# A convolution stage fed from strips of taps, with four images loaded side by side, logits in four column groups and a last batch scaled by two engines

## The chip, the cores and the metric

The kernel runs on one core of a Trainium2 chip. The core has four computing engines: TensorE (PE, matrix products; the profile lists its weight loads apart, as PEld), VectorE (DVE), ScalarE (ACT) and GpSimd (POOL), and SyncE (SP), which here issues most of the DMA transfers. Every engine takes its instructions strictly in the order of its own queue and waits on semaphores for the others. The metric is the device time of one execution in microseconds (us), lower is better. Before the change it is 16079.44 us, the median of three runs (16073.9 to 16081.61).

## What is computed

Two layers on `x` of shape (32, 128, 56, 56), all in float32. The change touches only the first lines of the first layer:

```python
x = conv_general_dilated(input, dw_kernel, (1, 1), ((3, 3), (3, 3)), feature_group_count=C) + dw_bias
x = transpose(x, (0, 2, 3, 1))                                   # one token of 128 channels per pixel
x = (x - mean(x)) / sqrt(var(x) + 1e-06) * ln_gamma + ln_beta    # over the channels
logits = x.reshape(T, C) @ Wg + bg                               # 8 experts
topv, topi = top_k(logits, 2)
...                                                              # routing, experts, and the second layer
```

So: a 7x7 convolution of each channel by itself, a normalization over the channels of each pixel, and eight logits per pixel, of which the two largest are found. Routing by priority with a capacity, the experts, and a second layer with a state-space scan follow.

## The kernel before

**Tiling.** The 32 images go in 8 batches of 4 (`NB0`). Rows of an image are taken in pairs: 2 rows of 56 pixels are 112 partitions (`TT`), and there are 28 pairs (`NP`). An image comes in with channels on partitions; `fill` (L341) loads it into one buffer `xt`, turns it with 29 transposes on PE (L349, `p_in`, four to a PSUM tile, two tiles) and ACT copies the result (L351) into `slots2`, of which there are two, for even and odd batches: [112 pixels, channel, image and row pair].

**Convolution.** `conv(b, c0)` (L353) does 4 channels of 4 images: for each channel four products (L379) over 112 pixels of an input row pair, with a 112 x 112 block of a band matrix that holds the 7x7 taps. 16 such matmuls are called a *group* here; a batch has 32 groups. A float32 matmul is two instructions on PE, each with its own weight load, so a group is 32 instructions. DVE adds the bias and writes back to `slots2` (L383); `pc` has three PSUM buffers. In the first batch the blocks are made: windows of the taps are loaded from `taps_d` with overlapping reads (`raw`, L361), copied by ACT to a dense form (L368), and stored by POOL's queue to `toep_d` (L369). Later batches load the dense form from there (L371, two loads of 392 KB per group, five buffers).

**Normalization.** `norm(b, i, q)` (L388) treats seven row pairs of one image; 16 calls make a batch. DVE takes statistics (L396, L398), ACT the root (L400), DVE the reciprocal and the shift `nm` (L401, L403). ACT scales seven times, one row pair each (L406: the *scalings*). POOL multiplies by gamma and adds beta (L409, L410) in `xa`, which has three buffers. SP stores `xa` to `res_d` (L412). PE turns `xa` (L420, seven transposes), ACT copies that (L422, two copies), PE computes the logits with seven products of 112 rows by 8 columns (L424), DVE adds the bias (L428). `top2` (L430) closes a batch on DVE.

**Order.** While batch b is convolved, batch b-1 is normalized and batch b+1 is filled. The loop over `k` at the end of the stage writes these calls in turn; a scheduler of the framework then orders the instructions of every engine when the program is built. Within an engine nothing changes at run time. After the last batch, 16 norms run with no convolution beside them. The stage ends with the last `top2`; routing, dispatch, experts and `layer1` (whose order is written out by hand in `PLAN` and `UNITS`) follow.

Of the kernel before, what the change touches and what calls it, by code (L numbers as in the profile page):

```python
# [5 lines left out]
F32 = mybir.dt.float32  # L6
# [14 lines left out]
E = 8  # L21
# [223 lines left out]
def tile_kernel(tc: tile.TileContext, a: dict, out: bass.AP):  # L245
# [14 lines left out]
    with (  # L260
# [43 lines left out]
        with (  # L304
# [4 lines left out]
            tc.tile_pool(name="po1", bufs=2, space=PSUM) as pot,  # L309
            tc.tile_pool(name="pl1", bufs=1, space=PSUM) as plg,  # L310
        ):
            wg = wp.tile([C, E], F32, name="wg")
            nc.sync.dma_start(out=wg, in_=a["L0_conv_Wg"])

            def rows(v, n, name):
                t = wp.tile([TT, n], F32, name=name)
                nc.sync.dma_start(out=t, in_=v.partition_broadcast(TT))
                return t

            bg = rows(a["L0_conv_bg"], E, "bg")  # L320
# [1 line left out]
            lng = rows(a["L0_conv_ln_gamma"], C, "lng0")  # L322
            lnb = rows(a["L0_conv_ln_beta"], C, "lnb0")

            taps_d = dram.tile([C, TR * TS], F32, name="taps_d")
            toep_d = dram.tile([TT, C, 8, HW], F32, name="toep_d")
            slots2 = [wp.tile([TT, C, NB0 * (NP + 1)], F32, name=f"xc{i}") for i in range(2)]  # L330

            xt = wp.tile([C, (HW + 2) * HW], F32, name="xt")
            nc.gpsimd.memset(xt, 0.0)
            taps = xt[:, : TR * TS].rearrange("c (y x) -> c y x", x=TS)
            dwk = a["L0_conv_dw_kernel"].rearrange("c o h w -> (c o) h w")
            for y in range(7):
                nc.sync.dma_start(out=taps[:, 7 - y, 52:59], in_=dwk[:, y, :])
            nc.sync.dma_start(out=taps_d, in_=xt[:, : TR * TS])
            nc.gpsimd.memset(xt[:, :HW], 0.0)

            def fill(b, i):  # L341

                n = b * NB0 + i
                nc.sync.dma_start(out=xt[:, HW : HW + L], in_=x_d[n])
                for j0 in range(0, NP + 1, 4):
                    w = min(4, NP + 1 - j0)
                    p = pin.tile([TT, 4, C], F32, name="p_in")
                    for j in range(w):
                        nc.tensor.transpose(p[:, j, :], xt[:, (j0 + j) * TT : (j0 + j + 1) * TT], ident)  # L349
                    o = i * (NP + 1) + j0  # L350
                    nc.scalar.copy(slots2[b % 2][:, :, o : o + w], p[:, :w, :].rearrange("p j c -> p c j"))  # L351

            def conv(b, c0):  # L353

                tp = []
                for c in range(c0, c0 + 4, 2):
                    t = cp.tile([TT, 2, 8, HW], F32, name="toep", bufs=5)
                    if b == 0:
                        raw = cp.tile([TT, 2, 8, TS], F32, name="raw", tag="xa", bufs=3)
                        for r in range(2):  # L360
                            nc.sync.dma_start(  # L361
                                out=raw[r * HW : (r + 1) * HW].rearrange("k c y x -> k c (y x)"),
                                in_=bass.AP(
                                    tensor=taps_d.tensor, offset=c * TR * TS + (1 - r) * TS,
                                    ap=[[1, HW], [TR * TS, 2], [1, 8 * TS]],
                                ),
                            )
                        nc.scalar.copy(t, raw[:, :, :, :HW])  # L368
                        nc.gpsimd.dma_start(out=toep_d[:, c : c + 2], in_=t)  # L369
                    else:  # L370
                        nc.sync.dma_start(out=t, in_=toep_d[:, c : c + 2])  # L371
                    tp.append(t)
                s4 = slots2[b % 2][:, c0 : c0 + 4, :].rearrange("p c (i j) -> p c i j", i=NB0)
                pc = pconv.tile([TT, 4, NB0, NP], F32, name="pc")
                for c in range(4):
                    for k, o in enumerate((1, 2, 0, 3)):

                        lo, hi = max(0, 1 - o), min(NP, NP + 2 - o)
                        nc.tensor.matmul(  # L379
                            pc[:, c, :, lo:hi], lhsT=tp[c // 2][:, c % 2, 6 - 2 * o : 8 - 2 * o, :],  # L380
                            rhs=s4[:, c, :, lo + o - 1 : hi + o - 1], start=k == 0, stop=k == 3,
                        )
                nc.vector.tensor_tensor(  # L383
                    s4[:, :, :, :NP].rearrange("p c i j -> p c i j"), pc,
                    dwb[:, c0 : c0 + 4].unsqueeze(2).unsqueeze(3).to_broadcast([TT, 4, NB0, NP]), ALU.add,
                )

            def norm(b, i, q):  # L388

                w = NP // 4  # L390
                o = i * (NP + 1) + q * w
                xv = slots2[b % 2][:, :, o : o + w]
                st = cp.tile([TT, w, 6], F32, name="st")
                mv = cp.tile([TT, w, 2], F32, name="mv")
                for j in range(w):
                    nc.vector.bn_stats(st[:, j, :], xv[:, :, j])  # L396
                for j in range(w):
                    nc.vector.bn_aggr(mv[:, j, :], st[:, j, :])  # L398
                rs = cp.tile([TT, w], F32, name="rs")
                nc.scalar.activation(rs, mv[:, :, 1], AF.Sqrt, bias=eps6[:TT])  # L400
                nc.vector.reciprocal(rs, rs)  # L401
                nm = cp.tile([TT, w], F32, name="nm")
                nc.vector.scalar_tensor_tensor(nm, mv[:, :, 0], -1.0, rs, ALU.mult, ALU.mult)  # L403
                xa = cp.tile([TT, 2 * 8 * TS], F32, name="xa", bufs=3)[:, : w * C].rearrange("p (j c) -> p j c", c=C)
                for j in range(w):
                    nc.scalar.activation(  # L406
                        xa[:, j, :], xv[:, :, j], AF.Identity, bias=nm[:, j : j + 1], scale=rs[:, j : j + 1]
                    )
                nc.gpsimd.tensor_tensor(xa, xa, lng.unsqueeze(1).to_broadcast([TT, w, C]), ALU.mult)  # L409
                nc.gpsimd.tensor_tensor(xa, xa, lnb.unsqueeze(1).to_broadcast([TT, w, C]), ALU.add)  # L410
                col = (b * NB0 + i) * TPI + q * w
                nc.sync.dma_start(  # L412
                    out=res_d[col * TT : (col + w) * TT, :].rearrange("(k p) c -> p k c", p=TT), in_=xa
                )
                pl = plg.tile([TT, w, E], F32, name="p_lg")
                for j0 in range(0, w, 4):
                    g = min(4, w - j0)
                    p = pot.tile([C, 4, TT], F32, name="p_xa")
                    for j in range(g):
                        nc.tensor.transpose(p[:, j, :], xa[:, j0 + j, :], ident[:TT, :TT])  # L420
                    xc = cp.tile([C, 4, TT], F32, name="xc_lg")
                    nc.scalar.copy(xc[:, :g, :], p[:, :g, :])  # L422
                    for j in range(g):
                        nc.tensor.matmul(pl[:, j0 + j, :], lhsT=xc[:, j, :], rhs=wg, start=True, stop=True)  # L424
                if i == 0 and q == 0:
                    lgs[b] = cp.tile([TT, NB0 * TPI, E], F32, name="lg")
                o = i * TPI + q * w
                nc.vector.tensor_tensor(lgs[b][:, o : o + w, :], pl, bg.unsqueeze(1).to_broadcast([TT, w, E]), ALU.add)  # L428

            def top2(b):  # L430

                n = NB0 * TPI
                big = [TT, n, E]
                cols = slice(b * n, (b + 1) * n)
                lg = lgs.pop(b)
                oh = cp.tile(big, F32, name="oh", bufs=1)
                first_b = first.unsqueeze(1).to_broadcast(big)
                v = cp.tile([TT, 2, n], F32, name="v", bufs=1)
                for k in range(2):
                    nc.vector.tensor_reduce(v[:, k, :], lg, AX.X, ALU.max)  # L440
                    nc.vector.tensor_tensor(oh, lg, v[:, k, :].unsqueeze(2).to_broadcast(big), ALU.is_equal)
                    nc.vector.tensor_tensor(oh, oh, first_b, ALU.mult)
                    nc.vector.tensor_reduce(picks[k][:, cols], oh, AX.X, ALU.max)
                    if k == 0:
                        nc.vector.tensor_tensor(
                            oh, first_b, picks[k][:, cols].unsqueeze(2).to_broadcast(big), ALU.is_equal
                        )
                        nc.vector.scalar_tensor_tensor(lg, oh, -3.0e38, lg, ALU.mult, ALU.add)
                nc.vector.tensor_tensor(less[:, cols], v[:, 1, :], v[:, 0, :], ALU.subtract)
# [992 lines left out]
```

## Time and profile before

| stretch of the profiled execution | us | what runs |
|---|---|---|
| 0 to 69 | 69 | constants, taps, four images loaded and turned |
| 69 to 249 | 180 | convolution of batch 0 |
| 249 to 1238 | 989 | batches 1 to 6: convolution, norms, fills |
| 1238 to 1390 | 152 | batch 7: convolution, norms of batch 6 |
| 1390 to 1535 | 145 | norms of batch 7 |
| 1535 to 16084 | 14549 | all the rest |

The profiled execution took 16086.15 us, with a span of 16084.4 us from its first to its last instruction on the core, at a mean granted TensorE clock of 0.888; the three unprofiled runs have their median at 16079.44 us. Over the span PE is busy for 13000.1 us, DVE 11071.4, ACT 11045.9, POOL 13580.1.

How to read the lines that follow: a timeline line has start, duration, engine, source line, operation, output <- inputs, shapes, and how often it follows itself; in brackets the idle time of the engine before it and what ended that. A row of a stretch has its bounds and length, the busy time of PE, PEld, DVE, ACT and POOL with the number of instructions, the granted TensorE clock as a share of full speed, the mean busy share of 16 DMA engines, and GB/s.

### The profile page before, as it was taken

How to read it: one execution, taken by the hardware profiler on the slowest of the kernel's cores; microseconds unless marked ns; L12 is line 12 of the kernel's file. 1: busy time of each engine (PE TensorE's matmuls, PEld its weight loads, DVE VectorE, ACT ScalarE, POOL GpSimd, SP SyncE). 2: the span in 40 equal slices, each digit the busy share in tenths (PEclk: the TensorE clock that was granted, in tenths of full speed). 3: DMA queues.
4: the chain of work that ended last, by engine and by line, in shares of the span. 5: the costliest groups of instructions: out<-in, count | busy, mean ns of one | idle time of the engine just before them, and what ended most of it. 6: DMA issues, size and time to landing. Idle time of an engine off the chain costs nothing. (4 is left out here: it accounts for less than half of the span.)

```text
span 16084.4 us, 247325 instructions
## 1 busy us (share of the span) xinstructions
PE 13000.1 (81%) x91637; PEld 7138.1 (44%) x91637; DVE 11071.4 (69%) x10582; ACT 11045.9 (69%) x23222; POOL 13580.1 (84%) x8121
## 2 busy tenths in 40 slices
PE   7996100001999989999999999999999999999998
PEld 6996100000777754444444444444444444444443
DVE  2655400000111139999999999999999999999999
ACT  4655200000444459999999999999999999999998
POOL 2443477777888879999999999999999999999999
PEclk9997555555999999999999999999999999999999
DMA  8785433332555545555555555555555555555555
GB/s 265 228 238 185 176 94 93 97 93 68 71 72 71 70 84 178 182 182 181 178 182 181 179 179 179 179 182 181 179 180 181 180 179 179 178 181 182 180 179 166
DMA packets 1239131, 2572.16 MB, mean 160 GB/s; under 512 B 139336, under 2 KB 676640, under 8 KB 1230240
## 3 DMA queue, kind: packets, MB, share of 16 engines
q1 hardware_dynamic: 1041440, 2361.89, 46.6%
q0 software_dynamic: 196480, 194.45, 7.0%
q8 instruction: 721, 11.81, 0.3%
q14 instruction: 490, 4.01, 0.1%
HBM read 2180.38 MB, written 375.43 MB: 159 GB/s over the span
## 5 line engine op out<-in xcount | busy, mean ns | idle before, releaser
L1326 POOL TENSOR_TENSOR db<-du,bb 128x896 f32<-128x896 f32 x3584 | 6835.8, 1936 | 24.8 <-DMA bb<-bc_d 21.8
L1339 ACT ACTIVATE da<-dt,aneg 128x449 f32<-128x449 f32 x7168 | 4534.9, 637 | 454.4 <-DVE prod L1377 297.4
L1357 DVE TENSOR_TENSOR_SCAN da<-da,db 128x898 f32<-128x898 f32 x2240 | 4525.4, 2020 | 157.9 <-ACT da L1339 157.2
L1286 PE MATMUL py<-prod,ident 64*64 64x448 f32 x28672 | 3279.1, 562 | 158.5 <-DVE prod L1377 150.9
L1377 POOL TENSOR_TENSOR prod<-hs,cb 128x896 f32<-128x896 f32 x1344 | 2603.9, 1937 | 153.8 <-issue 104.7
L1377 DVE TENSOR_TENSOR prod<-da,cb 128x896 f32<-128x896 f32 x2240 | 2439.3, 1089 | 233.2 <-PE py L1286 67.2
L944 ACT COPY xc<-ept 128x512 f32<-128x512 f32 (+1 forms) x248 | 143.9, 580 | 2916.5 <-PE ept L942 2614.5
L850 POOL DMA_INDIRECT buf_d<-xg,slot x1568 | 1641.9, 1047 | 538.4 <-issue 528.5
L902 POOL DMA_INDIRECT res_d<-ys,xb x984 | 1593.9, 1620 | 350.2 <-issue 287.3
L942 PE MATMUL ept<-ident,xb 128*128 128x128 f32 (+1 forms) x984 | 189.0, 274 | 2027.0 <-DMA xb<-buf_d 2023.2
L1286 PEld LDWEIGHTS py<-prod,ident 64*64 64x64 f32 x28672 | 1041.8, 134 | 1687.3 <-issue 969.6
L1357 DVE TENSOR_TENSOR_SCAN hs<-da,db 128x898 f32<-128x898 f32 x896 | 1785.6, 2014 | 0.1
L1122 PE MATMUL p_xm<-te,wk 128*128 128x448 f32 x3584 | 1416.0, 546 | 0.0
L894 DVE TENSOR_TENSOR ys<-py,b2t 128x512 f32<-128x512 f32 (+2 forms) x256 | 170.8, 670 | 1712.2 <-PE py L888 1541.6
L847 DVE COPY xg<-gate 128x28 f32<-128x28 f32 x56 | 12.7, 232 | 1896.2 <-DMA buf_d<-xg,slot 1896.2
L942 PEld LDWEIGHTS ept<-ident,xb 128*128 128x128 f32 (+1 forms) x984 | 124.6, 143 | 2030.7 <-issue 2026.3
L888 PEld LDWEIGHTS py<-w2t,hh 128*128 128x128 f32 x7872 | 938.8, 192 | 187.2 <-issue 113.1
L888 PE MATMUL py<-w2t,hh 128*128 128x128 f32 x7872 | 988.0, 279 | 11.0 <-ACT hh L884 10.7
L1122 PEld LDWEIGHTS p_xm<-te,wk 128*128 128x128 f32 x3584 | 657.5, 189 | 731.7 <-issue 567.3
L379 PE MATMUL pc<-xc,toep 112*112 112x112 f32 (+1 forms) x8192 | 937.4, 270 | 40.5 <-ACT toep L368 37.1
L1361 DVE TENSOR_TENSOR_SCAN hs<-da,db 128x449 f32<-128x449 f32 x896 | 924.9, 1074 | 1.3 <-ACT da L1339 0.9
L379 PEld LDWEIGHTS pc<-xc,toep 112*112 112x112 f32 x8192 | 880.7, 184 | 50.8 <-ACT toep L368 45.1
(238 smaller groups left out, 20802.2 us busy)
## 6 DMA issues: line engine op xcount, KB each, us to landing
cb<-bc_d SPq DMA_DIRECT2D x1792, 448.0 KB
bb<-bc_d SPq DMA_DIRECT2D x1792, 448.0 KB
toep<-toep_d SPq DMA_DIRECT2D x448, 392.0 KB
xg<-res_d SPq DMA_DIRECT2D x56, 1792.0 KB
buf_d<-zero SPq DMA_DIRECT2D x28, 2275.0 KB
xb<-buf_d SPq DMA_DIRECT2D x240, 260.0 KB
xt<-in_x SPq DMA_DIRECT2D x32, 1568.0 KB
res_d<-xa SPq DMA_DIRECT2D x128, 392.0 KB
```

Source lines behind the costliest of these rows:

```text
L379: nc.tensor.matmul(pc[:, c, :, lo:hi], lhsT=tp[c // 2][:, c % 2, 6 - 2 * o : 8 - 2 * o, :], rhs=s4[:, c, :, lo + o - 1 : hi + o - 1], star ...
L850: apart(nc.gpsimd.indirect_dma_start(out=buf_d[:, :], out_offset=bass.IndirectOffsetOnAxis(ap=slots[k][:, o + j : o + j + 1], axis=0), in_ ...
L888: nc.tensor.matmul(py[:n, j, :], lhsT=hh[:, k, j * 128 : j * 128 + n], rhs=w2t[:, k, :], start=k == 0, stop=k == KF - 1,)
L902: apart(nc.gpsimd.indirect_dma_start(out=res_d[:, :], out_offset=bass.IndirectOffsetOnAxis(ap=xb[:n, j, C + 1 : C + 2].bitcast(I32), axis= ...
L942: nc.tensor.transpose(pt[:, j * 128 : j * 128 + n], xb[:n, j, :C], ident[:n, :n])
L1122: nc.tensor.matmul(p[:, :CH1], lhsT=s["wk"][:, k, hs], rhs=d["te"][:, k : k + CH1], start=k == 0, stop=k == DC - 1 and not first,)
L1286: nc.tensor.matmul(ps[r][h * HD : (h + 1) * HD, :CH1], lhsT=lhsT(rs, h), rhs=rhs[rs, h, :], start=start, stop=stop,)
L1326: nc.gpsimd.tensor_tensor(dbv[i][:, :, 1:], st[g]["du"], units[u].pop("bb"), ALU.mult)
L1339: e = nc.scalar.activation(da[:, h * W1 : (h + 1) * W1], st[g]["dt"][:, h, :], AF.Exp, scale=s["aneg"][:, h, i : i + 1])
L1357: nc.vector.tensor_tensor_scan(hs, da, dbs[i], 0.0, ALU.mult, ALU.add)
L1361: half(u, h, nc.vector.tensor_tensor_scan(hs2[h][:, hh], da[:, hh], dbs[i][:, hh], 0.0, ALU.mult, ALU.add))
L1377: eng.tensor_tensor(w["prod"], w["hs"][0][:, :, 1:], w["cb"], ALU.mult)
```

## The change

Five things change in the stage:

- **Weights.** The dense form is gone. For every group of every batch two transfers load windows of the taps, 428 numbers for each of 56 partitions and 4 channels, straight from `taps_d` into one of three buffers `raws`; the second half of the partitions is shifted by one strip of 62 (`TS`), so that 118 neighbouring columns (`TM`) of the strip are the weights. The six columns between the two rows give six idle rows in the result. Everything behind has 118 partitions instead of 112, and `xa` is stored with two transfers per norm.
- **First images.** The four images of batch 0 are loaded into four places side by side in the second `slots2` buffer, which is free at that time.
- **Logits.** The two copies go to one buffer `turns`. Four products with `Wg` as weights (32 columns, 24 of them zero) and 224 moving columns write to four groups of 32 PSUM partitions; ACT copies the result (`lt`), two transposes turn it back, and DVE adds the bias.
- **Shift.** `nm` is computed by two operations on POOL instead of one on DVE.
- **Last batch.** Of the seven scalings of a norm of batch 7, DVE does three and ACT four.

```diff
+            whole = [wp.tile([128, C * NB0 * SH], F32, name=f"xc{i}") for i in range(2)]
+            TM = TS + HW
+            slots2 = [t[:TM].rearrange("p (c j) -> p c j", c=C) for t in whole]
...
+            begin = whole[1][:, : NB0 * PAD].rearrange("c (i n) -> c i n", i=NB0)
...
+            nc.sync.dma_start(out=begin[:, 0, HW : HW + L], in_=x_d[0])
+            nc.sync.dma_start(out=taps_d, in_=tapf)
+            raws = [wp.tile([TT, 4, 8, TS], F32, name=f"raw{i}") for i in range(3)]
...
+            def windows(c0):
+                t = raws[c0 // 4 % 3]
+                flat = t.rearrange("k c y x -> k c (y x)")
+                for r in range(2):
+                    nc.sync.dma_start(
+                        out=flat[r * HW : (r + 1) * HW, :, r * TS : r * TS + TN],
+                        in_=bass.AP(
+                            tensor=taps_d.tensor, offset=c0 * TR * TS + TS, ap=[[1, HW], [TR * TS, 4], [1, TN]],
+                        ),
+                    )
+                return flat
+            for i in range(1, NB0):
+                nc.sync.dma_start(out=begin[:, i, HW : HW + L], in_=x_d[i])
+            wg = wp.tile([C, 32], F32, name="wg")
+            turns = wp.tile([C, 8, TT], F32, name="xc_lg")
...
             def conv(b, c0):
-                for c in range(c0, c0 + 4, 2):
-                    t = cp.tile([TT, 2, 8, HW], F32, name="toep", bufs=5)
-                    if b == 0:
...
-                        nc.scalar.copy(t, raw[:, :, :, :HW])
-                        nc.gpsimd.dma_start(out=toep_d[:, c : c + 2], in_=t)
-                    else:
-                        nc.sync.dma_start(out=t, in_=toep_d[:, c : c + 2])
+                flat = windows(c0)
...
-                            pc[:, c, :, lo:hi], lhsT=tp[c // 2][:, c % 2, 6 - 2 * o : 8 - 2 * o, :],
+                            pc[:, c, :, lo:hi], lhsT=flat[:, c, (6 - 2 * o) * TS : (6 - 2 * o) * TS + TM],
...
-                nc.vector.scalar_tensor_tensor(nm, mv[:, :, 0], -1.0, rs, ALU.mult, ALU.mult)
+                nc.gpsimd.tensor_tensor(nm, mv[:, :, 0], rs, ALU.mult)
+                nc.gpsimd.tensor_scalar(nm, nm, -1.0, 0.0, ALU.mult, ALU.add)
+                xa = cp.tile([TM, w, C], F32, name="xa", bufs=3)
                 for j in range(w):
+                    if b == NB - 1 and j % 2:
+                        nc.vector.tensor_scalar(
+                            xa[:, j, :], xv[:, :, j], rs[:, j : j + 1], nm[:, j : j + 1], ALU.mult, ALU.add
+                        )
+                    else:
+                        nc.scalar.activation(
+                            xa[:, j, :], xv[:, :, j], AF.Identity, bias=nm[:, j : j + 1], scale=rs[:, j : j + 1]
                         )
...
+                for r in range(2):
+                    t0 = col * TT + r * HW
+                    nc.sync.dma_start(
+                        out=bass.AP(
+                            tensor=res_d.tensor, offset=t0 * C, ap=[[C, HW], [TT * C, w], [1, C]]
+                        ),
+                        in_=xa[r * TS : r * TS + HW],
                     )
...
-                    for j in range(g):
-                        nc.tensor.matmul(pl[:, j0 + j, :], lhsT=xc[:, j, :], rhs=wg, start=True, stop=True)
+                for j in range(4):
+                    nc.tensor.matmul(
+                        across[32 * j : 32 * j + 32], lhsT=wg, rhs=xc[:, 2 * j : 2 * j + 2, :], start=True, stop=True
+                    )
+                lt = cp.tile([128, 2, TT], F32, name="lt_lg")
+                nc.scalar.copy(lt, across)
+                for k in range(2):
+                    nc.tensor.transpose(back[:, k, :], lt[:, k, :], ident)
```

## The prediction

> **What bounds the kernel now.** I read the busy tenths of 40 slices first, then busy time by stage, then the timeline at the start of a batch and in mid batch.
>
> ```profile
> PE   7996100001999989999999999999999999999998
> ACT  4655200000444459999999999999999999999998
> POOL 2443477777888879999999999999999999999999
> PEclk9997555555999999999999999999999999999999
> ```
>
> A slice is 402 us. The change touches the first four alone, so the other 36 (routing, experts, the second layer, all with the same instructions) are taken as they are. Busy time of the engines by stretch:
>
> ```profile
> 69.00:249.00 180.00, 132.43 (x1141) 119.81 (x1140) 29.08 (x79) 74.41 (x96) 30.96 (x59) 0.97 0.93 318
> 249.00:1238.00 989.00, 951.78 (x8859) 922.95 (x8860) 555.14 (x1844) 583.75 (x1150) 401.28 (x192) 0.96 0.80 235
> 1390.00:1535.00 145.00, 69.66 (x337) 62.57 (x336) 75.17 (x282) 78.52 (x160) 66.38 (x32) 0.52 0.17 45
> 18.00:22.00 4.00, 2.55 (x12) 2.23 (x12) 0.00 (x0) 1.17 (x2) 0.00 (x0) 1.00 0.92 235
> ```
>
> Columns: length, then busy us of PE, PEld, DVE, ACT, POOL, granted clock, DMA share, GB/s. Batch 0 waits for DMA (0.93). Batches 1 to 6 take 165 us each and PE is busy in 96% of that. The tail without convolutions has no full engine: it is a chain. The last row is a stretch with tap windows alone in flight. Start of a batch, where norm 0 goes through ACT, POOL and back to PE:
>
> ```profile
> 581.01 3.90 ACT L406 ACTIVATE xa<-xc,nm,rs 112x128 f32<-112x128 f32 x7 [1.37 <-DVE nm L403]
> 584.99 2.08 POOL L409 TENSOR_TENSOR xa<-xa,lng 112x896 f32<-112x896 f32 x1 [34.50 <-ACT xa L406]
> 587.14 2.08 POOL L410 TENSOR_TENSOR xa<-xa,lnb 112x896 f32<-112x896 f32 x1
> 589.28 1.57 PE L420 MATMUL p_xa<-ident,xa 112*128 112x112 f32 x7 [3.24 <-POOL xa L410]
> ```
>
> PE stands 3.24 us for the transposes. The stretch after that, in the columns of the stages:
>
> ```profile
> 589.00:599.00 10.00, 9.72 (x52) 9.72 (x53) 6.31 (x31) 7.68 (x16) 6.12 (x4) 0.50 0.63 179
> ```
>
> The granted clock is 0.50 for 10 us. In mid batch nothing stands (the last two rows are from later stages, for two durations used below):
>
> ```profile
> 1333.10 0.83 PE L420 MATMUL p_xa<-ident,xa 112*128 112x112 f32 x7
> 1333.68 0.87 ACT L422 COPY xc_lg<-p_xa 128x448 f32<-128x448 f32 x2 [3.54 <-PE p_xa L420]
> 1333.77 0.56 PE L379 MATMUL pc<-xc,toep 112*112 112x112 f32 x4
> 1334.27 0.95 PE L424 MATMUL p_lg<-wg,xc_lg 128*112 128x8 f32 x8
> 1334.44 3.91 ACT L406 ACTIVATE xa<-xc,nm,rs 112x128 f32<-112x128 f32 x7
> 1335.86 5.93 PE L379 MATMUL pc<-xc,toep 112*112 112x108 f32 x58
> 1338.42 2.09 POOL L409 TENSOR_TENSOR xa<-xa,lng 112x896 f32<-112x896 f32 x1 [4.29 <-ACT xa L406]
> 1340.59 2.10 POOL L410 TENSOR_TENSOR xa<-xa,lnb 112x896 f32<-112x896 f32 x1
> ...
> 4203.96 0.83 PE L888 MATMUL py<-w2t,hh 128*128 128x128 f32 x6
> ...
> 9004.53 3.99 PE L1286 MATMUL py<-prod,ident 64*64 64x448 f32 x40
> ```
>
> While ACT copies (1333.68 to 1334.55), PE runs convolutions; the seven scalings that follow belong to a norm that PE wants three norms later. That lead keeps PE full.
>
> **The change, part by part.** The span is 16084.4 us; the profiled execution reports 16086.15, 6.7 above the median of the runs (16079.44).
>
> *Start.* The four first images came one after the other through one buffer; the first convolution stood at 69.46. Now image 0 is issued at about 0.8 and, as before, needs 7.7 us to its transposes (issued 11.71, used 19.45). By the build's order image 1 waits for image 0's semaphore, images 1 to 3 (4.8 MB, near 400 GB/s) land at about 24, and eight copies of 0.6 end at 30. So 30 (bounds 27 and 45).
>
> *Batch 0.* 64 copies `toep<-raw` (0.94 each) leave ACT, 64 DMA issues (0.53) leave POOL's queue. A convolution group (16 matmuls, 32 instructions) costs 32 x 0.0995 = 3.18 now ((5.93 - 0.26) / 57). The new weights have 118 columns. Eight logit products with 112 columns and only 8 moving ones go at (0.95 - 0.24) / 7 = 0.101, so columns set the pace; 128 columns (L888) take (0.83 - 0.27) / 5 = 0.112. 118 lies 6/16 of the way: 0.104, 3.33 a group. Batch 0 is 32 x 3.33 + 4 fills paced by 8 copies of 0.6 (4.9) = 126. DMA: 24.5 MB of windows at the 235 GB/s of the last row of stages is 104, plus 16 for 6.4 MB of images: 120. I take 130 (120 to 165). Batch 1 thus starts at 160, against 249.
>
> The Trainium skill, "DMA: Bandwidth & Descriptors", How many engines (k), speaks against this part: a transfer gets the largest number up to 16 that divides its slowest dimension, so 56 partitions get 14 engines where 112 got 16. By that, at 14/16 of batch 0's 318 GB/s, the windows would take 88 us a batch; the row's rate gives 104; neither passes what follows.
>
> *Batches 1 to 7.* Work on PE per batch: 32 x 3.33 = 106.6; fills 12.6; per norm seven transposes 0.7, logits in four groups, two more transposes 0.22. L1286 runs eight instructions of 448 columns on four parts of the array in 3.99 / 5 = 0.8, so 224 columns take about 0.45. Before, logits cost 14 x 0.101 = 1.4. Work alone would be 141, less than before (146).
>
> But the order decides. In the built program, PE's queue now reads, for two norms k, k+1 in mid batch, with ACT's beside it:
>
> ```
> PE   7 transposes k | 4 logits k | 2 back k | 16 conv | 3 transposes k+1 | 16 conv | 4 transposes k+1 | 4 logits k+1 ...
> ACT  2 copies k | copy lt k | 7 scalings k+1 | 2 copies k+1 ...
> POOL mult k+1 | nm k+3, first half | add k+1 | nm k+3, second half ...
> ```
>
> No convolution stands between transposes, logits and turning back, and the scalings of k+1 stand behind copy `lt` of k. Take 0 at the last transposes of k. Copies run 0.6 to 1.48 (as 1333.10 to 1333.68 to 1334.55), logits end at 2.1, `lt` (0.35: 448 columns 0.53, 336 0.44) at 2.5, PE is free at 2.8, after one group at 6.1. ACT: seven scalings 3.9, to 6.4. POOL: 0.07, then 4.24 for both operations (1338.42 to 1342.69 with the gap), one nm operation in between. Small POOL operations have no row; bounds 0.15 (a memset of 56 columns) and 1.2 (the nm of DVE beside POOL); I take 0.25, nearer the memset. So k+1 is ready at 11.05 and PE stands 4.9 us. Everything behind it on PE (16 convolutions, DVE's evictions of them, the statistics) is late, and so is the next round: the loop closes through PE itself.
>
> Going so through one whole batch of the order (norms 0 to 15):
> - one scaling behind `lt` (2 norms): 2.5 + 0.56 + 4.66 = 7.7 each, 15.4
> - three behind, or copies behind five (3): 9.7 + 8.9 + 8.9 = 27.5
> - seven behind, one more group between the transposes (3): 11.05 + 0.3 + 3.3 = 14.65 each, 43.9
> - the same behind a fill of 29 transposes (3): 17.8 + 23.2 + 17.7 = 58.7
> - logits split by a group (2): 16.5 + 11.7 = 28.2
> - norm 15 to the last convolution 2.8 + 6 x 3.33 + 4.9 = 27.8; from there to norm 0's transposes 1 + 2.4 + 0.5 + 0.9 (statistics, root) + 0.7 (nm) + 3.9 + 4.24 and gaps = 14.3, two groups inside; norms 0 to 2: 16.7.
>
> Together 232.5. Some eight waits per batch are over 4 us. After 3.24 us the row shows half clock for 10 us; that doubles a group (+3.3) or is swallowed by the chain: 0 to 26, I take 13. P = 245, against 165 (152 in batch 7, whose order without fills sums to 238).
>
> The Trainium skill, "TensorE: Matmul & The Clock Gate", Part 1, has the clock back after some 3.4 us of work, where the row shows 10. By the page the eight waits would cost 8 x 1.7 = 14, by the row up to 26.
>
> *Tail.* ACT keeps four of seven scalings, DVE takes three, nm leaves DVE (where it stood 1.1 behind POOL). POOL sets the pace: 4.24 + 0.5 = 4.75 a norm, against 8.0 (two norms in 16.03). 15 to the first, 15 x 4.9, 8 at the end: 98 (90 to 130) against 145.
>
> Evictions and additions over 118 rows instead of 112 cost nothing: rows lie side by side. A second store per norm is 0.32 on SP, where windows lead by three groups; without that lead each group would wait the landing.
>
> *Sum.* 30 + 130 + 7 x 245 + 98 = 1973 where 1535 stood: +438, 16084 + 438 = 16522 as a span, 16,515 beside the median.
>
> **The rivals.**
> - *The loop doesn't close* (scalings keep their lead, PE binds): 141 + 16 x 1.3 for the uncovered copies + 10 at the start = 172; 258 + 7 x 172 - 1535 = -73: 16,005. It decides below P = (1535 - 258) / 7 = 182. For it: all waits of PE on norms in 1 to 6 are 33 us of 989 today, ACT is busy 59%. Against: queues are in order, and the order has lost the lead. 0.13.
> - *The loop closes, but shorter*: no clock drops, nm at its low bound, part of the waits met by fills: P = 215, 16,310. 0.22.
> - *The four groups run one after another*: 1.5 for 0.45 in 16 links: +17 a batch, 16,635. Against: L1286. 0.07.
> - *Windows bind*: with packets of 1712 B instead of 1984 at two fifths of the row's rate, 260 + 41 for stores and images: P = 300, 16,900. Against: 235 GB/s at 0.92. 0.04.
>
> **How the numbers follow.** The forecast gets 0.54, its own range 16,420 to 16,610. The 80% range leaves out the first rival and the upper end of the last two: 16,200 to 16,680. A measurement of this kernel tells 0.2% (32 us) from no change; between the first rival and the shorter loop 0.02 falls there. Faster 0.12, slower 0.86.
>
> **What would show it.** First convolution near 30, batch 1 near 160. In batches 1 to 7: PE waits for `xa` of POOL of 4 to 5 us many times a batch, POOL waiting for ACT's scalings, ACT for `p_xa` and `p_lg`; clock well under 0.96; DMA share near 0.55; convolution pitch 0.104. Tail near 100 us. Wrong if the batches take under 182, if PE's waits name windows, or if scalings finish norms before PE asks.

## The result and the profile after

The changed kernel takes 16638.18 us (median of 4 runs, 16632.13 to 16641.87) against 16080.53 us before (16073.9 to 16081.83): ratio 1.0347, 95% interval 1.0331 to 1.0363. The prediction said 16,515 us, slower, 16,200 to 16,680. It forecast a loss of 435 us; the loss is 558. Its profiled execution has a span of 16640.1 us, against 16084.4 before.

The page of the changed kernel, busy tenths in 40 slices of 416 us:

```profile
PE   7777620000199999999999999999999999999998
ACT  3433330000044445999999999999999999999998
POOL 1222337777788887999999999999999999999999
PEclk8888755555599999999999999999999999999999
```

Before, PE reads 7, 9, 9 and 6 and its clock 9, 9, 9 and 7 in the first four slices; now PE is at 7, 7, 7, 7 and 6 and the clock at 8, 8, 8, 8 and 7, for five slices and not four. The changed kernel by stages (columns as before: length, busy us of PE, PEld, DVE, ACT, POOL, granted clock, DMA share, GB/s):

```profile
33.00:179.00 146.00, 128.88 (x1140) 121.18 (x1140) 28.19 (x74) 21.25 (x37) 0.43 (x2) 0.98 0.87 214
179.00:1713.00 1534.00, 1121.96 (x8472) 990.10 (x8473) 480.53 (x1753) 614.70 (x1247) 429.19 (x382) 0.84 0.56 147
1713.00:1980.00 267.00, 181.56 (x1294) 161.38 (x1293) 82.18 (x303) 85.77 (x177) 71.51 (x64) 0.79 0.47 114
1980.00:2094.00 114.00, 57.95 (x278) 31.61 (x276) 89.42 (x304) 58.96 (x128) 76.71 (x65) 0.55 0.22 57
2094.00:16640.00 14546.00, 11678.01 (x79831) 5874.72 (x79831) 10327.87 (x8058) 10211.34 (x21621) 13006.36 (x7791) 0.89 0.52 154
```

The last row, 14,546 us, was 14,549 before: the whole loss lies in the convolution stage, and in it in batches 1 to 7. A batch of 1 to 6 takes 255.7 us instead of 164.7. The second row tells what the 91 us are made of. PE idles (1534 - 1122) / 6 = 68.7 us a batch, against (989 - 951.8) / 6 = 6.2 before; and it is busy 1122 / 6 = 187.0 us against 158.6, though its work is no more than before: the granted clock is 0.84 instead of 0.96. Idle +62.5, slower work +28.4.

What PE waits for in batches 1 to 6 (the view of waits: engine, instruction, releaser, us in total, times, longest):

```profile
PE p_xa L445 <- POOL xa L430: 288.9, 86, 6.6
PE p_lg L455 <- ACT xc_lg L446: 49.2, 69, 4.1
PE p_lg L461 <- ACT lt_lg L459: 34.7, 78, 0.5
...
PE pc L393 <- DMA raw<-taps_d: 9.1, 6, 3.5
```

The same wait in the kernel before, over batches 1 to 7:

```profile
PE p_xa L420 <- POOL xa L410: 21.6, 6, 4.8
```

In the changed kernel windows are late six times in six batches; POOL's result is late 86 times in 96 norms. One round in mid batch, from the timeline:

```profile
799.73 0.45 ACT L446 COPY xc_lg<-p_xa 128x336 f32<-128x336 f32 x1
799.89 0.91 PE L455 MATMUL p_lg<-xc_lg,wg 128*32 128x224 f32 x8 [0.32 <-ACT xc_lg L446]
800.85 0.35 ACT L459 COPY lt_lg<-p_lg 128x224 f32<-128x224 f32 x1 [0.67 <-PE p_lg L455]
801.09 3.90 ACT L426 ACTIVATE xa<-xc,nm,rs 118x128 f32<-118x128 f32 x7
801.51 3.46 PE L393 MATMUL pc<-xc,raw 112*118 112x112 f32 x32
805.07 2.08 POOL L429 TENSOR_TENSOR xa<-xa,lng 118x896 f32<-118x896 f32 x1 [6.31 <-ACT xa L426]
807.27 2.09 POOL L430 TENSOR_TENSOR xa<-xa,lnb 118x896 f32<-118x896 f32 x1
809.41 0.85 PE L445 MATMUL p_xa<-ident,xa 118*128 118x118 f32 x3 [4.44 <-POOL xa L430]
810.05 5.60 PE L393 MATMUL pc<-xc,raw 112*118 112x112 f32 x32
```

ACT copies the logits `lt`, only then scales the next norm, POOL multiplies and adds, PE has done its one group long ago and stands 4.44 us, and the next group takes 5.60 instead of 3.46 us. Neither engine is short of capacity: ACT is busy 40% of the stage, POOL 28%.

### The profile page after: what moved, and what is told of

It reads as the page before. It is cut to its first block, busy times and chain, and to the rows that moved or that the text cites. A ratio compares the mean times of both kernels' runs of the same rounds, so it can differ in the third digit from the quotient of the medians.

```text
span 16640.1 us, 246555 instructions
## 1 busy us (share of the span) xinstructions
PE 13189.0 (79%) x91125; PEld 7193.6 (43%) x91125; DVE 11010.0 (66%) x10509; ACT 11011.6 (66%) x23239; POOL 13590.4 (82%) x8314
## 5 line engine op out<-in xcount | busy, mean ns | idle before, releaser
L429 POOL TENSOR_TENSOR xa<-xa,lng 118x896 f32<-118x896 f32 x128 | 266.5, 2082 | 1057.8 <-ACT xa L426 1057.1
L393 PE MATMUL pc<-xc,raw 112*118 112x112 f32 (+1 forms) x8192 | 1058.0, 298 | 34.6 <-DMA raw<-taps_d 17.8
L393 PEld LDWEIGHTS pc<-xc,raw 112*118 112x118 f32 x8192 | 1044.6, 215 | 44.8 <-issue 15.7
```

The costliest lines, as they stand in the source:

```text
L393: nc.tensor.matmul(pc[:, c, :, lo:hi], lhsT=flat[:, c, (6 - 2 * o) * TS : (6 - 2 * o) * TS + TM], rhs=s4[:TT, c, :, lo + o - 1 : hi + o - ...
```

## The experiments

The parts of a run are given as in the table: start (to the first convolution), batch 0, the mean of batches 1 to 6, batch 7, and the tail (last convolution to last logits), in us, from the trace; time is the median of the runs, and the ratio is to the kernel before on the same chip.

| run | start | batch 0 | 1 to 6 | 7 | tail | time | ratio (95%) |
|---|---|---|---|---|---|---|---|
| before | 69.5 | 180.0 | 164.7 | 152.1 | 144.7 | 16080.5 | |
| after | 33.4 | 145.8 | 255.7 | 267.4 | 112.8 | 16638.2 | 1.0347 (1.0331 to 1.0363) |
| e1 windows, old logits | 32.0 | 145.6 | 257.8 | 242.6 | 114.3 | 16634.4 | 1.0340 (1.0323 to 1.0357) |
| e2 dense, new logits | 69.2 | 183.1 | 170.3 | 150.1 | 122.9 | 16094.9 | 1.0009 (0.9999 to 1.0019) |
| e3 order by hand | 32.1 | 162.1 | 193.0 | 143.7 | 114.6 | 16161.1 | 1.0046 (1.0029 to 1.0063) |
| e4 split tail alone | 70.3 | 179.4 | 164.2 | 151.9 | 121.7 | 16054.9 | 0.9984 (0.9974 to 0.9994) |
| e5 hand, loads in quarters | 31.9 | 147.8 | 179.3 | 145.5 | 113.6 | 16067.2 | 0.9992 (0.9983 to 1.0002) |
| e6 lead of one | 32.2 | 146.7 | 218.6 | 200.5 | 172.0 | 16418.2 | 1.0210 (1.0193 to 1.0227) |
| e7 no products between | 32.0 | 146.2 | 192.6 | 159.9 | 114.6 | 16162.0 | 1.0050 (1.0033 to 1.0066) |
| e8 dense, start and tail | 36.4 | 194.5 | 164.8 | 151.5 | 121.8 | 16040.6 | 0.9975 (0.9965 to 0.9984) |
| e9 hand, lt first | 32.1 | 147.3 | 166.0 | 141.2 | 114.5 | 15993.9 | 0.9946 (0.9929 to 0.9963) |
| e10 two queues | 39.3 | 151.0 | 187.2 | 161.0 | 120.4 | 16159.6 | 1.0049 (1.0032 to 1.0066) |
| e11 half the windows | 32.0 | 124.9 | 174.7 | 153.5 | 120.5 | 16038.1 | 0.9971 (0.9960 to 0.9981) |
| e12 both moves | 32.5 | 148.0 | 221.3 | 188.1 | 172.0 | 16424.9 | 1.0214 (1.0197 to 1.0231) |

### Which part of the change brings the loop: e1, e2, e4

e1 is the changed kernel with the old logits and the old `nm`:

```diff
-                nc.gpsimd.tensor_tensor(nm, mv[:, :, 0], rs, ALU.mult)
-                nc.gpsimd.tensor_scalar(nm, nm, -1.0, 0.0, ALU.mult, ALU.add)
+                nc.vector.scalar_tensor_tensor(nm, mv[:, :, 0], -1.0, rs, ALU.mult, ALU.mult)
...
+                    xc = cp.tile([C, 4, TT], F32, name="xc_lg")
...
+                        nc.tensor.matmul(pl[:, j0 + j, :], lhsT=xc[:, j, :], rhs=wg[:, :E], start=True, stop=True)
```

> The changed kernel with two parts undone: the logits are again seven products of 112 rows by 8 columns, and nm is again one operation on DVE. Windows, side-by-side start and the split scalings of the last batch stay. Theory 'order' (the planned order that comes with the window loads closes the loop through ACT and POOL, whatever the logits look like): in the planned order the convolutions still come in blocks of 16 with transposes and logits side by side, only lt and the turning back are gone from the loop, about 1.1 us a norm or 18 us a batch, so a period of about 237 instead of 257 and 16,500 us (16,430 to 16,580). Theory 'logits' (the two added steps of the logits and nm on POOL made the loop): with both undone a batch takes at most 175 us, 16,070 or less. Theory 'weights' (window transfers or 118 columns hold the batches up): as the changed kernel, 16,600 to 16,640.

Measured: 16634.4 us, batches of 257.8. The logits and `nm` are not the cause. My own number missed too: without `lt` in the round I had expected 18 us less a batch, and nothing came off. Taken alone this fits the theory that the weights themselves cost the time; e5 decides that.

e2 is the reverse: the kernel before with the new logits, `nm` on POOL and the split scalings, on dense weights.

```diff
-                nc.vector.scalar_tensor_tensor(nm, mv[:, :, 0], -1.0, rs, ALU.mult, ALU.mult)
+                nc.gpsimd.tensor_tensor(nm, mv[:, :, 0], rs, ALU.mult)
+                nc.gpsimd.tensor_scalar(nm, nm, -1.0, 0.0, ALU.mult, ALU.add)
...
+                        across[32 * j : 32 * j + 32], lhsT=wg, rhs=xc[:, 2 * j : 2 * j + 2, :], start=True, stop=True
```

> The kernel before with three parts of the change: logits in four groups with lt and turning back, nm on POOL, scalings of the last batch split. Weights stay dense and the start is the old one. Theory 'order': with dense weights the planned order keeps convolutions between transposes, logits and turning back and scalings three norms ahead, so batches stay at 163 to 168 us, and only the tail changes, from 145 to about 112: 16,045 us (16,000 to 16,090). Theory 'logits': the loop comes with these edits, batches of 230 us or more, 16,450 or more. Theory 'weights' expects the same as 'order' here.

Measured: 16094.9 us, no loop. Of the 50 us above my number, 5.6 a batch (PE waits 32.7 us for `toep` in the stage, 1.4 before) and a tail of 122.9, not 112, make 45. The orders that the planner (the scheduler that sets each engine's order when the program is built) wrote for PE say why the loop is gone. X, G and T are transposes, logits and turning back of a norm, C a group with the number of its products that go together, I a fill:

```
after  X36x7 G36x4 T36x2 C101x16 X37x7 G37x4 T37x2 C102x16 X38x3 C103x16 X38x4 I16x8 G38 ...
e1     X36x3 C100x16 X36x4 G36x7 X37 C101x16 X37x6 G37x7 C102x16 X38x3 C103x16 X38x4 I16x8 ...
e2     X36x7 C106x2 G36x4 C106x5 T36x2 C106x9 X37x7 C107x2 G37x4 C107x5 T37x2 C107x9 C108x16 ...
```

With windows norm 36 meets group 100 or 101, with dense weights group 106, and only there do products stand between transposes, logits and turning back. It is the window loads that move the norms ahead in the plan.

e4 is the kernel before with the split scalings alone:

```diff
+                    if b == NB - 1 and j % 2:
+                        nc.vector.tensor_scalar(
+                            xa[:, j, :], xv[:, :, j], rs[:, j : j + 1], nm[:, j : j + 1], ALU.mult, ALU.add
+                        )
```

> The kernel before with the last part alone: in batch 7 DVE does three of seven scalings of a norm. Theory 'order' takes the parts as independent: the tail falls from 145 to 110 to 125 us, batches unchanged, 16,045 to 16,060 us. Rival: nm on DVE stands behind the new scalings and the chain per norm stays as long, tail 140 to 145, no change (16,075 to 16,085).

Measured: tail 121.7 instead of 144.7, 16054.9 us: this part pays 23 us by itself.

### Order or weights: e3, e5, e9

e3 has all of the change, but the stage is written in a fixed order: while norm `n` is scaled, norm `n - 3` is turned and its logits made.

```diff
+            def slot(n, it, first):
+                m = n - 3
+                    turn(m)
...
+                steps(it, 4)
+                    logits(m)
+                    scale(n, range(0, 7) if first else range(1, 7))
...
+                steps(it, 5)
+                    back(m)
+                steps(it, 16)
...
+                with tc.manual_schedule():
```

> All of the change, the same operations, but the order of the convolution stage is written out by hand: scalings of norm n go out with the transposes of norm n - 3, four products of a group stand between transposes and logits, five more between logits and turning back, and a fill has two products after each four transposes. Theory 'order': PE stays fed, a batch takes 150 to 165 us, and with a start of 34, a batch 0 of 146 and a tail of 105 to 115 the kernel takes 15,900 to 16,010 us. Theory 'logits' (the longer chain is too long in any order): a batch of 200 us or more, 16,230 or more. Theory 'weights': window transfers and wider weights cost the same in any order, 235 us or more a batch, 16,490 or more.

Measured: 16161.1 us, batches of 193.0 with fills, 143.7 without (batch 7). Neither theory's number: the order gives back 62.7 us a batch, but PE now waits 111.6 us for windows. They stand behind whole images in SP's queue; batch 7, which loads none, takes 143.7, near PE's busy time of 137. (In this run windows of the last two groups of a batch were replaced too early, so some products had other weights.)

e5 takes the buffers in running order, loads images in quarters, and stores after the group:

```diff
-                t = raws[c0 // 4 % 3]
+                t, c0 = raws[K % 3], K % 32 * 4
...
+                m = L // 4
+                for k in range(4):
+                    nc.sync.dma_start(
+                        out=xt[:, HW + k * m : HW + (k + 1) * m], in_=x_d[b * NB0 + i][:, k * m : (k + 1) * m]
+                    )
+                    yield
```

> The order by hand again with three corrections: the three window buffers are taken by the running number of the group (in the run before, the windows of the last groups of a batch were overwritten early, so those products had other weights), an image is loaded in quarters with a group between them, and the stores of a norm are issued after the group and not ahead of it. In the run before, 111.6 us of PE's waits were for windows, which stood behind whole images of 1.57 MB. Theory 'order': with that gone only the bytes are left as a floor, 24.0 MB of windows, 6.4 of images and 6.3 of stores a batch at 235 GB/s or 156 us, near PE's own 142; 158 to 172 us a batch and 15,950 to 16,020 us. Rival 'weights': the windows are late whatever is done about the images, 185 us or more a batch, 16,120 or more.

Measured: 16067.2 us, batches of 179.3. Between the two numbers, but the question is decided: the same operations on the same bytes, in another order, take 571 us less than the changed kernel and as long as the kernel before. PE's waits in this run (195 to 1350 us, same columns):

```profile
PE p_lg L503 <- ACT lt_lg L495: 74.2, 30, 5.7
PE p_lg L491 <- ACT xc_lg L482: 51.9, 21, 6.0
PE pc L400 <- DMA raw<-taps_d: 11.8, 15, 2.1
```

Windows are down to 11.8 us. What is left is ACT: the first scaling of a slot waits for a buffer of `xa` that is still being stored, and `lt` stands behind it. ACT's own waits in the same stretch:

```profile
ACT xa L455 <- DMA res_d<-xa: 122.6, 39, 6.6
```

e9 puts `lt` ahead of the scalings, the first roots of a batch behind `lt`, and the stores back at the start of a slot:

```diff
-                if s_ok and not first:
-                    scale(n, range(0, 1))
...
                     logits(m)
...
-                    scale(n, range(0, 7) if first else range(1, 7))
+                    scale(n, range(0, 7))
```

> As e5 with the order of ACT mended where e5 shows PE waiting for it (126 us for the copies and lt in batches 1 to 6, most of it in the slots after a fill and at the first norm of a batch): lt goes out ahead of all seven scalings, the first roots of a batch behind lt, and the stores at the start of a slot. Theory 'order': these waits go, about 18 us a batch, and a batch takes 160 to 168 us: 15,940 to 16,000 us. Rival 'weights': DMA (share 0.82 in e5) takes over, 172 to 180 us a batch, 16,010 to 16,070 us.

Measured: 15993.9 us, batches of 166.0. Ratio to the kernel before 0.9946 (0.9929 to 0.9963): this version beats both, the kernel before by 0.5%. That gain lies in start, batch 0, batch 7 and tail; batches 1 to 6 take 166.0 us, no less than the 164.7 before. The order by hand was not tried on dense weights. Its stages (180 to 1175 are batches 1 to 6, then batch 7):

```profile
180.00:1175.00 995.00, 907.20 (x8413) 841.42 (x8413) 493.68 (x1780) 622.43 (x1239) 453.42 (x384) 0.97 0.87 226
1175.00:1316.00 141.00, 134.27 (x1295) 125.52 (x1295) 84.67 (x299) 84.70 (x176) 78.03 (x64) 0.99 0.88 219
```

PE's busy time is 907.20 us for six batches where the changed kernel needed 1121.96 for nearly as many instructions, and the clock is 0.97. DMA is at 0.87: the bytes of the windows may be the next bound, as the rival of this run said, but PE waits only 26.8 us for them in these six batches. From a norm's logits to the products behind its turning back in this kernel:

```profile
826.09 0.81 PE L491 MATMUL p_lg<-xc_lg,wg 128*32 128x224 f32 x8
826.84 1.28 PE L400 MATMUL pc<-xc,raw 112*118 112x112 f32 x10
826.95 0.35 ACT L495 COPY lt_lg<-p_lg 128x224 f32<-128x224 f32 x1 [0.67 <-PE p_lg L491]
827.96 0.38 PE L503 MATMUL p_lg<-ident,lt_lg 128*112 128x128 f32 x2
828.18 4.96 PE L400 MATMUL pc<-xc,raw 112*118 112x112 f32 x46
```

None of PE's lines has a bracket: the products after the logits cover `lt`.

### Which half of the order: e6, e7, e12

e6 keeps the products between the steps and takes the lead away: the scalings of norm `n` go out behind `lt` of norm `n - 1`. With it go things that the lines below don't show: the norms stand evenly over the batch, the seven scalings go out together, and the stores go out with the transposes. e9 also has all seven together and issues its stores early, and loses nothing by it; the even spread was not tested by itself.

```diff
-                m = n - 3
+                m = n - 1
```

> As e5 with one thing moved: the scalings of norm n go out behind the copy lt of norm n - 1 and not of norm n - 3; products still stand between transposes, logits and turning back. Theory 'lead' (PE waits because the scalings of the next norm stand behind lt of this one): the round 2.5 + 3.9 + 4.24 + 0.4 = 11 us a norm closes again, against some 8 of work, and the clock falls with the waits: 200 to 250 us a batch, 16,230 to 16,570 us. Theory 'blocks' (PE waits because no product stands between transposes, logits and turning back): as e5.

Measured: 218.6 us a batch, 16418.2 us, and a tail of 172.0 instead of 113.6, for the lead of one goes through the tail too. PE waits again for POOL (195 to 1350 us):

```profile
PE p_xa L481 <- POOL xa L462: 235.3, 64, 6.0
PE p_lg L491 <- ACT xc_lg L482: 27.4, 5, 5.7
```

e7 keeps the lead and takes the products away:

```diff
-                steps(it, 4)
+                steps(it, 0)
...
-                steps(it, 5)
+                steps(it, 0)
```

> As e5 with one thing moved: transposes, logits and turning back of a norm follow each other on PE with no product between; the scalings keep their lead of three norms. Theory 'lead': PE waits only for ACT's copies and for lt, 1.3 + 1.2 us a norm or 40 us a batch, part of it hidden in what e5 waits for DMA: 180 to 200 us a batch, 16,100 to 16,230 us. Theory 'blocks': these waits make most of the loss, 230 us or more, 16,430 or more.

Measured: 192.6 us a batch, 16162.0 us. The lead, with what goes with it in e6, is worth 39 us a batch, the products 13.

e12 has both edits.

> e6 and e7 together: scalings of norm n behind lt of norm n - 1, and no product between transposes, logits and turning back; a regular form of what the planner wrote for the changed kernel, without its transposes split around a group. If the two parts add, a batch takes 180 + 38 + 12 = 230 us (225 to 238) and the kernel 16,370 to 16,470 us. If they make the whole loss of the changed kernel, 250 to 260 us and 16,560 to 16,640. If the lead alone sets the round (11 us a norm whatever stands on PE), as e6, 215 to 222 and 16,400 to 16,430.

Measured: 221.3, 16424.9 us: the parts don't add; once the lead is gone, what stands between the steps hardly matters. But 221.3 isn't 255.7. The spacing of the norms tells the rest. From the first transposes of a batch's norm 0 to those of its norm 15 (15 steps), and from norm 15 to norm 0 of the next batch, means over batches 1 to 5 in the traces:

| run | norm 0 to 15 | 15 to next 0 |
|---|---|---|
| before | 136.0 | 29.7 |
| after | 206.9 | 48.0 |
| e9 | 161.7 | 4.9 |
| e12 | 203.9 | 17.6 |

From norm 0 to norm 15 both need about the same time, 204 and 207 us, with the plainest steps at 10.7 us in both. But in that time PE runs 31 groups in e12 and idles 32 us, and only 23 groups in the changed kernel, where it idles 60. The other nine groups stand behind norm 15 and make most of the 48.0 us; PE idles 8 of them. So the other 30 us are where the planner put the norms: they run ahead of their groups, each waits for the one before, and they leave the last groups of a batch without a norm beside them.

### What the planner answers to: e10, e11

e10 is the changed kernel with one line edited:

```diff
-                    nc.sync.dma_start(
+                    (nc.sync, nc.gpsimd)[r].dma_start(
                         out=flat[r * HW : (r + 1) * HW, :, r * TS : r * TS + TN],
```

> The changed kernel with one line edited: the second of the two window transfers of a group is issued by POOL instead of SP. The planner alone orders the stage; its order for PE now has products between transposes, logits and turning back, and most norms come about 5 groups later than in the changed kernel. Theory 'order': the time follows the planned order, 165 to 185 us a batch, 16,000 to 16,130 us. Rival 'queue': the loads stand in POOL's queue between the multiplication and the addition and wait there for a buffer, so the additions are late and the loop closes again, 210 us or more a batch, 16,300 or more. Rival 'bytes': as the changed kernel, since the same bytes move, 16,600 to 16,640.

Measured: 16159.6 us, batches of 187.2: 479 us less than the changed kernel for one line, and a little above my range. For these norms the plan is that of dense weights again ("X36x7 C106x2 G36x4 C106x5 T36x2 C106x9 ..."). What remains is partly the rival's: between 195 and 1300 us POOL stands 269.3 us for `raw` buffers that products hold, and PE 28.7 us for windows.

e11 leaves out the second of the two window transfers of each group, and with it the terms of the second row of each pair:

```diff
-                for r in range(2):
+                for r in range(1):
```

> The changed kernel without the second window transfer of each group, so the products lack the terms of the second row of each pair; all instructions but those 256 transfers stay. The planned order turns back to products between transposes and logits. Theory 'order': 152 to 168 us a batch, a batch 0 near 115 to 146, 15,880 to 16,000 us. Theory 'weights' would have the batches shrink with the bytes of the windows, 24.0 to 12.0 MB: from 257 to some 170 us if windows bound them, 16,050 or so; so the two differ little here, and the clock and PE's waits tell: under 'order' PE's waits for windows are small in both kernels.

Measured: 16038.1 us, batches of 174.7, the plan again as with dense weights, and PE waits 0.5 us for windows between 195 and 1300 us. The number is 7 us a batch above my range, through waits for fills and POOL. The time alone would also fit the theory of weights (16,050); what speaks against it is the changed kernel, where PE waits 9.1 us for windows in six batches. Together: two window transfers a group on SP's queue make the planner set the norms early; one, or one on each of two queues, does not. That it reckons the queue to be the bound is the likely reason, but no run shows the planner's own reckoning.

### The start on dense weights: e8

The kernel before with the images side by side and the split scalings:

```diff
+            begin = whole[1][:, : NB0 * PAD].rearrange("c (i n) -> c i n", i=NB0)
...
+                    img = begin[:, i, :]
```

> The kernel before with two parts of the change: the four first images side by side, and the split scalings of the last batch. Weights, logits, nm as before. Theory 'order' takes the parts as independent: first convolution near 40 instead of 69.5, tail 122 as measured for the split alone, batches unchanged: 16,025 us (16,010 to 16,040). Rival: batch 0 is bound by DMA (share 0.94 before), so that an earlier start is given back by the end of batch 0: 16,050 to 16,060.

Measured: 16040.6 us. Both sides have a share: the first convolution comes 33.1 us earlier, and batch 0, with a DMA share of 0.93, gives 14.5 of it back. This, too, beats the kernel before, with none of the rest of the change.

## Why the prediction was right, and where its sizes were off

**The mechanism was right.** The loop from `lt` through scalings and POOL back to PE is in the timeline, and e5 against e6 shows it as a cause. The plain round takes 10.7 us where the prediction had 11.05. DMA share (0.56 for "near 0.55"), waits, clock below 0.96 and a convolution pitch of 0.104 ((3.46 - 0.26) / 31 = 0.103) came as written. The measured 16,638 lies above the forecast's own 16,420 to 16,610; every term of the table below was too small, so nothing cancelled.

**What it did not see is where the order came from.** It read the order off the plan and gave no cause for it; that `lt` stands in the loop made it look like a matter of the logits. e1 shows that the loop stays without `lt`, e2 that the logits bring no loop. It is the windows, through the plan.

**Term by term** (the two rows of norms count from a norm's last transposes, as the prediction's list does):

| step | predicted | measured |
|---|---|---|
| start | 30 | 33.4 |
| batch 0 | 130 | 145.8 |
| norms 0 to 15 of a batch | 190.4 + 13 for the clock | 210.1 |
| norm 15 to the next 0 | 42.1 | 44.7 |
| batches 1 to 7, mean | 245 | 257.4 |
| tail | 98 | 112.8 |

The difference of 121 us is 7 x 12.4 = 87 from the batches, 16 from batch 0, 15 from the tail and 3 from the start.

- *The clock was under-priced.* The prediction took eight drops a batch of 10 us each and let half of their 26 us be swallowed. The trace's record of the granted clock has 66 stretches at half clock in batches 1 to 6, 11 a batch, 474.5 us of 1534 in all. 40 of them last 6.8 us, 12 last 3.4, 11 last 10.2. So the prediction's row of 10 us was the long end, and the 3.4 us after which the Trainium skill, "TensorE: Matmul & The Clock Gate", Part 1, has the clock back, the short one. At 79 us a batch the time at half clock is the 80 that were foreseen; the share of it that counts was set too low. In one batch (norms 32 to 47) the short rounds take 7.5 us (7.7 predicted), but those with one group between the transposes 16.5 to 17.1 (14.65), those behind a fill 20.6, 26.3 and 18.1 (17.8, 23.2 and 17.7), and the two with split logits 18.3 and 15.4 (16.5 and 11.7). That the clock alone makes the difference is likely, not shown. Batch 7, at 238 in the prediction, took 267.4 at a granted clock of 0.79.
- *Batch 0:* PE's work was sized well (128.9 busy for 126); of the 17 us beside it only 4 were in the sum. PE waits 11 us of them for windows and images, at a DMA share of 0.87 and 214 GB/s. How many DMA engines a window transfer used, no run here shows.
- *The tail:* the pace of POOL was right (33.4 + 33.8 us for 32 operations, 0.45 for `nm`), but it does not set the pace alone. POOL waits 26.2 us for ACT, nine times, and eight of these times ACT's last scaling stands behind a copy of the norm before: the loop of the batches runs here too, and that is the term which the prediction left out of the tail. One such wait, from POOL's addition for one norm to its multiplication for the next:

```profile
2037.51 2.08 POOL L430 TENSOR_TENSOR xa<-xa,lnb 118x896 f32<-118x896 f32 x1
...
2040.53 1.19 PE L445 MATMUL p_xa<-ident,xa 118*128 118x118 f32 x5
...
2041.22 1.03 ACT L446 COPY xc_lg<-p_xa 128x448 f32<-128x448 f32 x2 [1.63 <-PE p_xa L445]
...
2042.14 0.65 ACT L426 ACTIVATE xa<-xc,nm,rs 118x128 f32<-118x128 f32 x1
2042.88 2.08 POOL L429 TENSOR_TENSOR xa<-xa,lng 118x896 f32<-118x896 f32 x1 [3.06 <-ACT xa L426]
```

- *The small costs* held: `nm` on POOL 0.20 + 0.21 (0.25 each), eight logit instructions 0.59 us in e9 where PE doesn't wait among them (0.45), so that the four groups do run together and that rival falls. (In the changed kernel the second half mostly waits for the second copy, and the eight take 0.91 or more.)

**The rivals.** "The loop doesn't close" was priced at 172 us a batch and 16,005 us. It did not happen in the changed kernel, but with the order mended it does: 166.0 and 15,994 (e9). The shorter loop (215 a batch, no drop of the clock) did not come: 257.4, with 11 drops. Windows as the bound: not at a DMA share of 0.56.

**Slips in the prediction's figures** that change nothing: its 33 us of waits on norms are those of batches 1 to 7 (1 to 6: 25.3); the tail's 15 + 15 x 4.9 + 8 make 96.5, not 98; and POOL's two operations with their gap take 4.27 us, not 4.24.

## What to carry to other kernels

Where a planner orders the instructions, a change of loads can be a change of order: read the planned order of the busiest engine before and after, and if it moved, try the same operations in the old order (or a load on another queue) before judging the change. In a chain that passes several in-order engines, what keeps the busy one fed is how many rounds ahead the other engines' work for it is issued, here three; a lead of one closes the loop even with ACT busy 48% of the time and POOL 35% (e6). A large change may hold parts that pay by themselves (here the start and the tail): measure each alone.

## What the hardware showed beside that

DVE's scalings in the tail, taking turns with POOL's multiplications and additions (timeline of the changed kernel):

```profile
2042.88 2.08 POOL L429 TENSOR_TENSOR xa<-xa,lng 118x896 f32<-118x896 f32 x1 [3.06 <-ACT xa L426]
2043.47 3.79 DVE L422 TENSOR_SCALAR xa<-xc,rs,nm 118x128 f32<-118x128 f32 x2
2045.04 2.08 POOL L430 TENSOR_TENSOR xa<-xa,lnb 118x896 f32<-118x896 f32 x1
2047.32 0.40 DVE L422 TENSOR_SCALAR xa<-xc,rs,nm 118x128 f32<-118x128 f32 x1
```

A scaling takes 0.40 us when POOL stands. Eighteen of the 48 run into a multiplication or addition of POOL and end 0.15 us after it does: the two here take 1.64 and 2.23 us. The group in the tail (instructions, busy us and mean ns, idle before) has a mean of 915 ns:

```profile
L422 DVE TENSOR_SCALAR xa<-xc,rs,nm 118x128 f32<-118x128 f32 x48 | 41.6, 915 | 7.8 <-POOL nm L418 7.8
L410 DVE BATCH_NORM_STATS2 st<-xc 118x6 f32<-118x128 f32 x112 | 38.0, 403 | 0.0
...
L429 POOL TENSOR_TENSOR xa<-xa,lng 118x896 f32<-118x896 f32 x16 | 33.4, 2090 | 26.8 <-ACT xa L426 26.2 <-issue 0.5
```

The statistics of the same engine show nothing of the kind: 0.41 us with POOL working or not. The Trainium skill, "SBUF — State Buffer", Who interferes with whom, has this: DVE and GpSimd share a pair of ports as an exclusive lock, and `tensor_scalar` is among the operations that can take it. The trace agrees, with 0.40 and 2.23 us. None of POOL's nine waits for ACT was for such a scaling, though: DVE's had each time ended at least 1.2 us before ACT's last one. What DVE's late work on the statistics behind them costs the tail was not measured apart.
